# Shared expert's split weights kept on chip, matmul operands placed modulo 512 bytes, and later sends in a fused two-layer kernel

## The chip, the core and the metric

The kernel runs on one NeuronCore of one Trainium2 chip. The metric is device time in microseconds (us) of one execution. A core has a matrix engine (TensorE, PE in the profile; its weight loads are PEld), a vector engine (VectorE, DVE), a scalar engine (ScalarE, ACT), GpSimd (POOL) and SyncE (SP). The last three also issue DMA transfers, each in its own queue. Each engine works through its own queue in order and waits for semaphores of the others. On-chip memory has 128 partitions; a matmul reads a stationary operand of 128x128 and a moving one of up to 512 columns from it, and writes to PSUM.

## The reference

`x` is 32 sequences of 128 tokens with 512 features. Two layers, each a "cond" part that feeds an "ffn" part:

```
# layer 0, cond: mixture of experts with one shared expert
shared = (silu(x @ sw1.T) * (x @ sw3.T)) @ sw2.T            # hidden 1024
s      = sigmoid(x @ router_w.T + t_emb @ router_t_w.T)     # 8 experts, best 2 of them
routed = sum over the 2 chosen: gate * (gelu(x @ rw1[e].T) @ rw2[e].T)   # hidden 256
hid    = (shared + routed) / 3
# layer 0, ffn: each sequence picks one of 8 experts from its last token
sel    = argmax(softmax(gelu(hid[:, -1] @ Wp1 + bp1) @ Wp2 + bp2))
x1     = x + hid + 0.3 * ((gelu(hid @ W1[sel] + b1) @ W2[sel] + b2) @ Wo + bo)
# layer 1, cond: token shift, 16 experts by a hash of the token id, capacity 256 each
xk, xr = x1 + (shift(x1) - x1) * maa_k,  x1 + (shift(x1) - x1) * maa_r
y      = relu(buf @ w_key[e])**2 @ w_value[e], gathered back
r      = sigmoid(xr @ w_recept.T)
# layer 1, ffn: a gated recurrence over the 32 sequences (batch: 128 positions)
c      = sigmoid(z@wf.T + c@uf.T + bf) * c + sigmoid(z@wi.T + c@ui.T + bi) * tanh(z@wc.T + c@uc.T + bc)   # z = r * y
out    = x1 + tanh(z @ wo.T + c_final @ uo.T + bo)
```

All of it is float32.

## The kernel before, in words

**Matmuls in three terms.** Every float32 operand of a large matmul is split into a high part (a cast on ACT, L62) and a low part (a subtraction on DVE, L63), by `split`. `mm3` (L65 to L74) then issues three matmuls for each 128 of the contraction: high·high, high·low, low·high. So a product over 512 features is 12 matmuls.

**Stages, in order of time.** (1) *Shared expert, groups 0 to 3*: a group is 4 sequences, 512 tokens. `shared` (L193) loops over units `n`, eight per group (one per 128 of the hidden 1024): `up(n)` makes two products of 12 matmuls with 512 columns (`p`, from `xhl` and `swu`), `down(n - 1)` 12 matmuls into four accumulators (`acc`, from `swd` and `as`). For each unit the three raw weights are fetched by SP (`fetch_sw`, 256 KB each, tiles `swr`) two units ahead and split (`split_sw`) one unit ahead into two rotating buffers, although the same eight units of weights come round in each group. Router, top-2 choice and slot numbers run beside it. (2) *Routed experts*: 71 blocks of 128 gathered tokens; `r_up` (`pur`, 12 matmuls of 256 columns), `turn_h`, `r_down` (`por`, 6 of 512), with the split weights `r1`, `r2` (64 KB per partition each) in the right-hand memory. Near its end (`i == NBLK - 10`, block 61) the first `x` and the first two weight units of the next stage are fetched and split. (3) *Shared expert, groups 4 to 7*: the same loop (`shared` again, L926), with `combine` for finished sequences between (`sums`): POOL gathers two routed rows (`o`), DVE adds, PE transposes (`pth`), ACT scales. In group 7 DVE runs `policy` (which expert each of the first 24 sequences takes), POOL gathers the first expert weights (`fetch_w`, tiles `rawB`), and `split_w` splits them into four tiles `wB_W1a`, `wB_W1b`, `wB_W2a`, `wB_W2b`.

(4) *The sequences' experts*: the loop at L1131, one sequence per iteration, in order of their expert, so that weights change seldom. PE does `up` in two halves (`pu`), `bend` (transposes and gelu), `turn_r` (transposes of the sequence before into `rT`), and `down` in two halves (`po`). Every second iteration a pair of sequences is closed: `close(c)` multiplies with `Wo` (`pb`, 48 matmuls of 256 columns), forms `x1`, `dx`, `xk`; `mix_r(c)` makes `xr`. `send_k(b)` transposes `xk` and stores its rows, `send_v(b)` multiplies `xr` with `w_recept` (`pv`, 12 matmuls) and stores the result. (5) *16 experts*: `phD` (256 columns, from `xe` and `wD`) and `poD` (512 columns, from `wD` and `hD`). (6) *Recurrence*: 32 steps, each with three products of the state (`uc`, `ui`, `uf` with `cT`), three of the input (`wc`, `wi`, `wf` with `z`) and a part of the output product (`poF`).

**Where tiles lie.** Tile pools are stacks: left-hand pools grow up from the constants, right-hand pools down from the top of the memory. The last constant is `pad`, 64 bytes (L137). `shifted` (L56) gives a tile 128 bytes more than it needs and starts its use 64 bytes in; `xb`, `rT` and `xe`, which meet 256-column matmuls, are made by it.

**Order in queues.** The program's order is the base; the tile framework's planner then orders each engine's queue by its own costs and due times, so work that isn't ready in its plan is placed behind other work. `reuse_waits="tile"` makes a new tile wait for the last users of the bytes it takes.

Of the kernel before, what the change touches and what calls it, by code (L numbers as in the profile page):

```python
# [42 lines left out]
LINE = 128 // 4  # L43
SHIFT = LINE // 2


@with_exitstack
def tile_kernel(ctx: ExitStack, tc: tile.TileContext, a: dict, out: bass.AP):
# [7 lines left out]
    def shifted(pool, n, **kw):  # L56

        return pool.tile([P, n + LINE], FR, **kw)[:, SHIFT : SHIFT + n]

# [77 lines left out]
    pad = const.tile([P, SHIFT], F32, name="pad")  # L137
# [7 lines left out]
    with ExitStack() as sa:  # L145
        kw = dict(reuse_waits="tile")
        raw_p = sa.enter_context(tc.tile_pool(name="raw_p", bufs=6, **kw))
        swu = sa.enter_context(tc.tile_pool(name="swu", bufs=2, **kw))
        swd = sa.enter_context(tc.tile_pool(name="swd", bufs=2, **kw))
        xh = sa.enter_context(tc.tile_pool(name="xh", bufs=KD, **kw))  # L150
        xgp = sa.enter_context(tc.tile_pool(name="xgp", bufs=3, **kw))
# [6 lines left out]

        NSW = KF * NG
        sw_raw, sw_hl, x_raw, xhl = {}, {}, {}, {}  # L160

        def fetch_sw(n, which=range(3)):
            if n < NSW:
                sw_raw.setdefault(n, {}).update(
                    {i: fetch(a["sw"][n % KF, i], f"swr_{n}_{i}") for i in which}
                )

        def split_sw(n, which=range(3)):
            if n < NSW:
# [23 lines left out]
        def shared(groups, pools, hook, done, mid=None, before_last=None, more=False):  # L193
# [36 lines left out]
            for n in range(first, last + 1):  # L230
# [11 lines left out]
                if c == KF - 2 and (g < groups[-1] or more):  # L242
                    fetch_x(g + 1)
# [7 lines left out]
        with ExitStack() as s0:  # L251
# [22 lines left out]
            s1, ps_x, ps_u = ExitStack(), None, None  # L274
            srt = s0.enter_context(ExitStack())
# [304 lines left out]
            def hook2(g, c):  # L580
# [4 lines left out]
                if g == 1 or (g == 2 and c < 5):  # L585
# [3 lines left out]
                    if g == 2 and c == 4:  # L589
# [5 lines left out]
                        r12.append(rw_p.tile([P, 2, E0 * RCOL], FR, name="r1"))  # L595
                        r12.append(rw_p.tile([P, 2, E0 * RCOL], FR, name="r2"))
# [30 lines left out]
        with s1:  # L627
# [37 lines left out]
            for i in range(NBLK + 1):  # L665
# [8 lines left out]
                if i == NBLK - 10:  # L674
                    with tc.issue_after(stored):
                        fetch_x(NG // 2)
                    split_x(NG // 2)
                    fetch_sw(NSW // 2)
                    split_sw(NSW // 2)
                    fetch_sw(NSW // 2 + 1)  # L680

        srw.close()

        wh = sw_.enter_context(tc.tile_pool(name="wh", bufs=1, side="right", **kw))
# [143 lines left out]
        ws = {k: wh.tile([P, 2, KD, D], FR, tag="w" + k, name=f"wB_{k}") for k in ("W1a", "W1b", "W2a", "W2b")}  # L828
# [23 lines left out]
        def split_w(i):  # L852

            if i < len(todo):
                raw = raws.pop(i)
                kind, b = order[todo[i]]
                if b not in (0, PARTS[0]) and b not in changed:
# [12 lines left out]
        with ExitStack() as s2:  # L870
            tp = s2.enter_context(tc.tile_pool(name="tp2", bufs=2, **kw))
# [57 lines left out]
    with ExitStack() as sb:  # L929
# [4 lines left out]
        wb = sb.enter_context(tc.tile_pool(name="wb", bufs=1, **kw))  # L934
        sc = sb.enter_context(ExitStack())
# [20 lines left out]
        seqs = {}  # L956
# [68 lines left out]
        def turn_r(b):  # L1025
# [5 lines left out]
            if j == 0:  # L1031
                rT = shifted(bp, 2 * KD * PB * P, tag="rT", name=f"rT_{c}")
                rTs[c] = rT.rearrange("p (h k q) -> p h k q", h=2, k=KD)
# [9 lines left out]
        def close(c, last=False):  # L1043
# [4 lines left out]
            x1 = bp.tile([P, -(-n1 // LINE) * LINE], F32, tag="x1", name=f"x1_{c}")  # L1048
# [42 lines left out]
        def mix_r(c, pool, tag):  # L1091
# [6 lines left out]
            xrs[c] = pool.tile([P, 2, KD, PB, P], FR, tag=tag, name=f"xr_{c}")  # L1098
# [32 lines left out]
        for b in range(-1, NB + 1):  # L1131
# [25 lines left out]
            if b + 1 < NB:  # L1157
                bend(b + 1, "a")
                up(b + 1, "b")
                used()  # L1160
            if late == GB and step == 2:
                sc.close()
                end_p = sb.enter_context(tc.tile_pool(name="end_p", bufs=1, **kw))
            if b == NB:
                send_v(NB - 6)
            if j == PB - 1 and 0 <= c < NB // PB:
# [6 lines left out]
            if 0 <= b < NB:  # L1173
                down(b, "b")
                used()
            if b + 1 < NB:
                bend(b + 1, "b")
            if 0 <= b - 2 < NB - 2:
                send_k(b - 2)
                if b - 2 < NB - 6:  # L1180
                    send_v(b - 2)
# [488 lines left out]
```

## Time and profile before

| | |
|---|---|
| median of 3 runs | 2561.73 us (2558.79 to 2566.84) |
| the profiled execution | 2564.9 us, of it span 2563.2 us |
| granted TensorE clock, mean | 0.988 |
| PE busy in the span | 2480.9 us |
| DMA moved | 370.01 MB |

| stage | us from the span's start |
|---|---|
| 1 shared expert, groups 0 to 3 | 5 to 307 |
| 2 routed experts | 307 to 558 |
| 3 shared expert, groups 4 to 7 | 558 to 863 |
| 4 sequences' experts | 863 to 1495 |
| 5 16 experts | 1495 to 1867 |
| 6 recurrence and output | 1867 to 2563 |

The stages are cut at the first matmul of each kind in the timeline of PE. A row of a timeline gives start, duration, engine, line, operation, out<-in, shape and count, and in brackets how long the engine had been idle and what ended that. A row of the waits gives the waiting group, the group waited for, the total in us, how often, and the longest. Matmuls are pipelined: the distance from one start to the next is what one costs, and the duration in a row is longer than that. A name in the profile has its numbers left out.

### The profile page before, as it was taken

The page shows a single profiled execution, that of the slowest core. Times are in us where ns is not written, and L with a number is a line of the kernel's source. Part 1 is how long each engine was busy: PE and PEld are TensorE (multiplying, and loading weights), DVE is VectorE, ACT ScalarE, POOL GpSimd, SP SyncE. Part 2 cuts the span into 40 slices and gives each one's busy share as a digit, 9 for nine tenths or more (in the row PEclk, how much of TensorE's full clock was granted, in tenths as well). Part 3 has the DMA queues.
Part 4 walks back from the last instruction along what each step waited for, and adds up shares of the span by engine and source line. Part 5 has one row for each costly group of instructions (what it writes and reads, how often), then busy time and mean ns, then how long its engine had stood idle before and what let it go on. Part 6 is the DMA issues. An engine that isn't in the chain of part 4 may idle for free. (4 is left out here: it accounts for less than half of the span.)

```text
span 2563.2 us, 37388 instructions
## 1 busy us (share of the span) xinstructions
PE 2480.9 (97%) x13044; PEld 2076.7 (81%) x13044; DVE 1374.6 (54%) x2413; ACT 1104.7 (43%) x2007; POOL 437.8 (17%) x459
## 2 busy tenths in 40 slices
PE   8999999999997998999999999999999999999996
PEld 5788899987876787888887889999978888888885
DVE  7797655557767544445454477667643332333336
ACT  5445533344445544455455466666532222222214
POOL 1000022222323223333222110000010000000003
PEclk9999999999998999999999999999999999999998
DMA  5445544477777324333243287776451111111027
GB/s 179 161 132 176 169 155 151 155 230 244 268 255 246 119 87 128 100 117 111 81 139 120 93 280 241 230 228 223 140 168 42 38 37 37 37 42 46 25 74 267
DMA packets 203487, 370.01 MB, mean 144 GB/s; under 512 B 38625, under 2 KB 73489, under 8 KB 200225
## 3 DMA queue, kind: packets, MB, share of 16 engines
q1 hardware_dynamic: 151872, 263.30, 30.6%
q0 software_dynamic: 36160, 74.90, 9.9%
q10 hardware_dynamic: 15264, 29.37, 3.1%
q8 instruction: 108, 1.77, 0.3%
q14 instruction: 83, 0.67, 0.1%
HBM read 392.81 MB, written 88.13 MB: 188 GB/s over the span
## 5 line engine op out<-in xcount | busy, mean ns | idle before, releaser
L70 PE MATMUL p<-xhl,swu 128*128 128x512 f32 x1536 | 380.7, 401 | 17.9 <-DVE sg L211 7.7
L70 PEld LDWEIGHTS p<-xhl,swu 128*128 128x128 f32 x1536 | 290.4, 192 | 81.6 <-issue 8.1
L63 DVE TENSOR_TENSOR wD<-rawD,wD 128x1024 fp32r<-128x1024 f32 x128 | 156.5, 1229 | 78.6 <-ACT wD L62 78.5
L70 PE MATMUL acc<-swd,as 128*128 128x512 f32 x768 | 188.2, 392 | 2.1 <-ACT as L62 1.2
L70 PEld LDWEIGHTS phD<-xe,wD 128*128 128x128 f32 x1536 | 184.5, 190 | 1.3
L70 PE MATMUL phD<-xe,wD 128*128 128x256 f32 x1536 | 185.2, 281 | 0.0
L70 PE MATMUL poD<-wD,hD 128*128 128x512 f32 x768 | 182.7, 393 | 0.0
L70 PEld LDWEIGHTS acc<-swd,as 128*128 128x128 f32 x768 | 143.6, 188 | 34.3 <-ACT as L62 2.1
L70 PEld LDWEIGHTS poD<-wD,hD 128*128 128x128 f32 x768 | 142.0, 188 | 29.6 <-DVE hD L63 0.4
L62 ACT CAST wD<-rawD 128x1024 fp32r<-128x1024 f32 x128 | 133.1, 1047 | 55.3 <-PE poD L70 30.7
L255 POOL DMA_INDIRECT xg<-in_x_rows_dram,blk_t x71 | 67.5, 951 | 466.1 <-PE ptx L265 261.6
L1352 POOL DMA_INDIRECT y<-res_d,gat_i x32 | 32.3, 1009 | 583.1 <-DVE r L1371 504.1
L70 PE MATMUL por<-r,hbr 128*128 x426 | 117.7, 410 | 3.0 <-ACT hbr L62 2.9
L70 PE MATMUL pur<-r,xb 128*128 x852 | 118.7, 288 | 0.2
L63 DVE TENSOR_TENSOR xb<-ptx,xb 128x512 fp32r<-128x512 f32 x71 | 49.1, 691 | 112.6 <-ACT xb L62 112.6
L62 ACT CAST swu<-swr 128x512 fp32r<-128x512 f32 x128 | 75.0, 620 | 79.4 <-PE p L70 52.6
L70 PEld LDWEIGHTS pur<-r,xb 128*128 128x128 f32 x852 | 105.6, 189 | 2.0 <-ACT xb L62 0.6
L70 PE MATMUL pv<-w_recept_hl,xr 128*128 128x512 f32 x384 | 100.2, 406 | 5.9 <-DVE xr L63 5.9
L708 POOL DMA_INDIRECT o<-o_d,s_i x64 | 78.8, 1232 | 150.8 <-DVE swu L63 28.8
L70 PE MATMUL ps_f<-wf_hl,z 128*128 128x512 f32 x384 | 98.0, 402 | 1.7 <-ACT wf_hl L62 0.8
L70 PE MATMUL ps_c<-wc_hl,z 128*128 128x512 f32 x384 | 96.6, 399 | 0.7 <-ACT z L62 0.7
L70 PEld LDWEIGHTS pb<-rT,Wo_hl 128*128 128x128 f32 x768 | 92.8, 188 | 4.7 <-DVE rT L1037 3.2
(1005 smaller groups left out, 4856.8 us busy)
## 6 DMA issues: line engine op xcount, KB each, us to landing
swr<-in_sw_dram SPq DMA_DIRECT2D x192, 256.0 KB
rawD<-in_w_key_dram SPq DMA_DIRECT2D x64, 512.0 KB
rawD<-in_w_value_dram SPq DMA_DIRECT2D x64, 512.0 KB
o_d<-obr SPq DMA_DIRECT2D x71, 256.0 KB
xraw<-in_x_dram SPq DMA_DIRECT2D x32, 256.0 KB
rraw<-in_rw_dram SPq DMA_DIRECT2D x32, 256.0 KB
xc<-in_x_dram SPq DMA_DIRECT2D x32, 256.0 KB
hid_d<-o ACTq DMA_DIRECT2D x32, 256.0 KB
```

The costliest lines, as they stand in the source:

```text
L62: nc.scalar.copy(hi, src)
L63: return nc.vector.tensor_tensor(lo, src, hi.bitcast(F32), ALU.subtract).ins
L70: done = nc.tensor.matmul(ps, lhsT=left(hl, k), rhs=right(hr, k), start=start and k + n == 0, stop=stop and 3 * k + n == last,)
L255: nc.gpsimd.indirect_dma_start(out=xg[i], out_offset=None, in_=a["x_rows"], in_offset=bass.IndirectOffsetOnAxis(ap=blk_t[:, i : i + 1], ax ...
L708: nc.gpsimd.indirect_dma_start(out=o[n], out_offset=None, in_=o_d, in_offset=bass.IndirectOffsetOnAxis(ap=idx[:, b : b + 1], axis=0),)
L1352: nc.gpsimd.indirect_dma_start(out=y, out_offset=None, in_=res_d, in_offset=bass.IndirectOffsetOnAxis(ap=gat_i[:, b : b + 1], axis=0),)
```

## The change

Three things. **Kept weights**: in group 4 the split weights of the eight units go into four tiles `kept_u` and two tiles `kept_d`, and groups 5 to 7 read them there; no weight is fetched or split after unit 39. `kept_u` takes the four slots that the sequences' weights (`wB_*`) take over later, tile by tile; `kept_d` has a pool of its own on the right. `swu` and `swd` exist in stage 1 alone. `x` of groups 6 and 7 is fetched at `c == 3`, not 6. The first `x` of stage 3 is fetched at block 55, not 61, and the first kept weights are split after stage 2, not in it. `r2` is allocated ahead of `r1`, so they change places. **Addresses**: `pad` has 448 bytes, `shifted` adds 512 bytes and starts 64 bytes in, `x1` and `rT` get pools of their own behind the others. **Later sends**: `close` and `mix_r` stand at the end of the iteration, and both sequences of a pair are sent in the iteration after it, their pieces between `up`, `down` and `bend`.

```diff
-LINE = 128 // 4
-SHIFT = LINE // 2
+LINE, SHIFT, RIGHT = 512 // 4, 64 // 4, 480 // 4
...
-    def shifted(pool, n, **kw):
-        return pool.tile([P, n + LINE], FR, **kw)[:, SHIFT : SHIFT + n]
+    def shifted(pool, n, by=SHIFT, **kw):
+        return pool.tile([P, n + (LINE if by == SHIFT else by)], FR, **kw)[:, by : by + n]
...
-    pad = const.tile([P, SHIFT], F32, name="pad")
+    pad = const.tile([P, 448 // 4], F32, name="pad")
...
-        swu = sa.enter_context(tc.tile_pool(name="swu", bufs=2, **kw))
-        swd = sa.enter_context(tc.tile_pool(name="swd", bufs=2, **kw))
...
-        xgp = sa.enter_context(tc.tile_pool(name="xgp", bufs=3, **kw))
+        sxg = sa.enter_context(ExitStack())
+        xgp = sxg.enter_context(tc.tile_pool(name="xgp", bufs=3, **kw))
...
         NSW = KF * NG
+        KEPT = KF * (NG // 2)
...
         def fetch_sw(n, which=range(3)):
-            if n < NSW:
+            if n < KEPT + KF:
...
         def split_sw(n, which=range(3)):
-            if n < NSW:
+            if n >= KEPT:
+                c = n % KF
+                if n < KEPT + KF:
+                    if c % 2 == 0:
+                        kept_u[c // 2] = wh.tile([P, 2, 2, 2, KD, P], FR, tag="w", name=f"kept_u{c}")
+                    if c % 4 == 0:
+                        kept_d[c // 4] = dn_p.tile([P, 4, 2, D], FR, tag="d", name=f"kept_d{c}")
+                sw_hl[n] = kept_u[c // 2][:, c % 2], kept_d[c // 4][:, c % 4]
+            if n < KEPT + KF:
...
-                if c == KF - 2 and (g < groups[-1] or more):
+                if c == (KF - 2 if n < KEPT + KF else 3) and (g < groups[-1] or more):
                     fetch_x(g + 1)
...
-                        r12.append(rw_p.tile([P, 2, E0 * RCOL], FR, name="r1"))
-                        r12.append(rw_p.tile([P, 2, E0 * RCOL], FR, name="r2"))
+                        r12[:] = [rw_p.tile([P, 2, E0 * RCOL], FR, name=n) for n in ("r2", "r1")][::-1]
...
-                if i == NBLK - 10:
+                if i == NBLK - 16:
                     with tc.issue_after(stored):
                         fetch_x(NG // 2)
+                if i == NBLK - 10:
                     split_x(NG // 2)
-                    fetch_sw(NSW // 2)
-                    split_sw(NSW // 2)
-                    fetch_sw(NSW // 2 + 1)
+                    fetch_sw(KEPT)
+                    fetch_sw(KEPT + 1)
+        sxg.close()
         srw.close()
-        wh = sw_.enter_context(tc.tile_pool(name="wh", bufs=1, side="right", **kw))
+        wh = sw_.enter_context(tc.tile_pool(name="wh", bufs=4, side="right", **kw))
...
-        ws = {k: wh.tile([P, 2, KD, D], FR, tag="w" + k, name=f"wB_{k}") for k in ("W1a", "W1b", "W2a", "W2b")}
+        ws = {}
...
+                if b == 0:
+                    ws[kind] = wh.tile([P, 2, KD, D], FR, tag="w", name=f"wB_{kind}")
...
+            dn_p = s2.enter_context(tc.tile_pool(name="dn_p", bufs=2, side="right", **kw))
+            split_sw(KEPT)
+            pad2 = dn_p.tile([P, 320 // 4], F32, bufs=1, name="pad2")
+            nc.gpsimd.memset(pad2, 0.0)
...
+        x1p = sb.enter_context(tc.tile_pool(name="x1p", bufs=1, **kw))
+        rTp = sb.enter_context(tc.tile_pool(name="rTp", bufs=1, **kw))
...
-                rT = shifted(bp, 2 * KD * PB * P, tag="rT", name=f"rT_{c}")
-                rTs[c] = rT.rearrange("p (h k q) -> p h k q", h=2, k=KD)
+                rTs[c] = rTp.tile([P, 2, KD, PB * P], FR, tag="rT", name=f"rT_{c}")
...
-            x1 = bp.tile([P, -(-n1 // LINE) * LINE], F32, tag="x1", name=f"x1_{c}")
+            x1 = x1p.tile([P, n1 - n1 % LINE + SHIFT], F32, tag="x1", name=f"x1_{c}")
...
-            xrs[c] = pool.tile([P, 2, KD, PB, P], FR, tag=tag, name=f"xr_{c}")
+            if pool is not end_p:
+                xrs[c] = pool.tile([P, 2, KD, PB, P], FR, tag=tag, name=f"xr_{c}")
+            else:
+                xr = shifted(pool, 2 * KD * PB * P, LINE - SHIFT, tag=tag, name=f"xr_{c}")
+                xrs[c] = xr.rearrange("p (h k b q) -> p h k b q", h=2, k=KD, b=PB)
...
             if b + 1 < NB:
                 bend(b + 1, "a")
+            pair = b - 3 if b % 2 and 0 <= b - 3 < NB - 2 else None
+            if pair is not None:
+                send_k(pair)
+            if b + 1 < NB:
                 up(b + 1, "b")
                 used()
...
+            if pair is not None:
+                send_k(pair + 1)
             if b == NB:
                 send_v(NB - 6)
+            if 0 <= b < NB:
+                down(b, "b")
+                used()
+            if pair is not None and pair < NB - 6:
+                send_v(pair)
+            if b + 1 < NB:
+                bend(b + 1, "b")
+            if pair is not None and pair < NB - 6:
+                send_v(pair + 1)
             if j == PB - 1 and 0 <= c < NB // PB:
                 wo_done, k_done = close(c, b == NB)
                 fetch_xh(c + 1)
...
-            if 0 <= b < NB:
-                down(b, "b")
-                used()
-            if b + 1 < NB:
-                bend(b + 1, "b")
-            if 0 <= b - 2 < NB - 2:
-                send_k(b - 2)
-                if b - 2 < NB - 6:
-                    send_v(b - 2)
...
-            mix_r(NB // PB - 1, bp, "rT")
+            mix_r(NB // PB - 1, rTp, "rT")
```

More of the change, by code (lines that the diff above doesn't have):

```diff
@@ L159, in tile_kernel @@
         NSW = KF * NG
+        KEPT = KF * (NG // 2)
         sw_raw, sw_hl, x_raw, xhl = {}, {}, {}, {}
+        kept_u, kept_d = {}, {}
         def fetch_sw(n, which=range(3)):
-            if n < NSW:
+            if n < KEPT + KF:
                 sw_raw.setdefault(n, {}).update(
@@ L274, in tile_kernel @@
             s1, ps_x, ps_u = ExitStack(), None, None
+            swu = s0.enter_context(tc.tile_pool(name="swu", bufs=2, **kw))
+            swd = s0.enter_context(tc.tile_pool(name="swd", bufs=2, **kw))
             srt = s0.enter_context(ExitStack())
@@ L954, in weight_b @@
             return pair
-        seqs = {}
+        seqs, end_p = {}, None
         def seq(p):
```

## The prediction

> **What bounds the kernel now.** I read the page's busy times first, then who waited for whom on TensorE, then the timeline of single stages. The page:
>
> ```profile
> PE 2480.9 (97%) x13044; PEld 2076.7 (81%) x13044; DVE 1374.6 (54%) x2413; ACT 1104.7 (43%) x2007; POOL 437.8 (17%) x459
> ```
>
> TensorE (PE) is the bound all through; the other engines matter only where PE waits for them. So a gain has two sources: a shorter matmul, or a PE wait that goes. Matmul spacing first, in one step of the last recurrence (start, duration, group):
>
> ```profile
> 2102.78 2.88 PE L70 MATMUL ps_c<-uc_hl,cT 128*128 128x512 f32 x12
> 2105.50 2.88 PE L70 MATMUL ps_i<-ui_hl,cT 128*128 128x512 f32 x12
> 2108.22 2.95 PE L70 MATMUL ps_f<-uf_hl,cT 128*128 128x512 f32 x12
> 2111.01 2.96 PE L70 MATMUL ps_c<-wc_hl,z 128*128 128x512 f32 x12
> 2113.81 2.97 PE L70 MATMUL ps_i<-wi_hl,z 128*128 128x512 f32 x12
> ```
>
> Same shape, but start to start the first two take 2.72 us per 12 (226.7 ns each), uf 2.79, wc 2.80. What differs is the addresses, which follow from adding up the tiles. Left-hand pools begin at 20064, 96 modulo 512; right-hand pools end at 229344, 480. uc, ui and cT are left (96 and 96); uf and the three input weights are right (480 against 96).
>
> PE's waits in the second shared stage (557.8 to 863.3 us):
>
> ```profile
> PE p L70 <- DVE sg L211: 7.7, 1, 7.7
> PE p L70 <- DVE xhl L63: 3.4, 2, 2.1
> PE pth L728 <- ACT o L730: 3.1, 1, 3.1
> ```
>
> and among the sequences' experts (863 to 1495 us):
>
> ```profile
> PE pv L70 <- DVE xr L63: 5.9, 2, 3.0
> PE ptB L1105 <- DVE xk L1059: 4.7, 3, 2.1
> PE pb L70 <- DVE rT L1037: 3.0, 1, 3.0
> ```
>
> They cost more than they last. PE in the first:
>
> ```profile
> 770.38 0.47 PE L70 MATMUL p<-xhl,swu 128*128 128x512 f32 x1
> 772.96 4.32 PE L70 MATMUL p<-xhl,swu 128*128 128x512 f32 x11 [2.11 <-DVE xhl L63]
> 780.35 1.12 PE L728 MATMUL pth<-ident,o 128*128 128x128 f32 x4 [3.06 <-ACT o L730]
> 781.12 3.91 PE L70 MATMUL p<-xhl,swu 128*128 128x512 f32 x12
> 784.86 1.52 PE L70 MATMUL acc<-swd,as 128*128 128x512 f32 x6
> ```
>
> 11 matmuls in 4.32 us: after a wait, seven to ten run at 427 ns, half clock. From 770.38 to 784.86 are 14.5 us for two groups of 12 and four transposes, worth 5.8: 8.7 us lost. Behind it, on ScalarE (ACT) and GpSimd (POOL):
>
> ```profile
> 771.07 0.62 ACT L62 CAST xhl<-xraw 128x512 fp32r<-128x512 f32 x1 [3.71 <-DMA xraw<-in_x_dram]
> ...
> 778.66 0.62 ACT L62 CAST swu<-swr 128x512 fp32r<-128x512 f32 x1 [3.30 <-DMA swr<-in_sw_dram]
> ...
> 821.89 1.05 ACT L62 CAST wB_W1a<-rawB 128x1024 fp32r<-128x1024 f32 x1 [8.21 <-DMA rawB<-in_W1a_dram,idxw]
> 814.74 1.62 POOL L837 DMA_INDIRECT rawB<-in_W1a_dram,idxw  x1 [0.31 <-DVE condS L804]
> ```
>
> ACT stands in order before a transfer, and what PE needs is queued behind. At 821.89 that transfer is the first sequence's weights, gathered once VectorE (DVE) has finished the policy; with the half clock 12.8 us go between 814.8 and 832.0.
>
> **The change, 1: addresses.** The pad of 448 for 64 bytes moves the left pools from 96 to 480. Every tile behind it is a multiple of 512 or, with x1 and rT, comes last, so 512-column operands agree. Per 12 matmuls the recurrence gains 0.07 (uf), 0.08 (wc), 0.09 (wi) and 0.05 (wf: 2.88 against 2.83 for poF, both behind transposes): 0.29 x 32 steps = 9.3 us. Among the sequences' experts (weights 480, activations 96 or 352; timeline from 1050 to 1067) groups take 2.77 to 2.79, 2.88 behind transposes, against 2.72 and 2.83: 0.055 x 128 = 7.0. Routed down (por, mean start to start 232.4 ns against about 227.5): 426 x 5 ns = 2.1. The value matmuls that use the left-hand pool in the 16-expert stage: 256 x 5 = 1.2. Together 19.6.
>
> The 256-column matmuls keep a difference, now 64 bytes. phD at a difference (stationary less moving) of 448 takes 117.8 ns today, at 320 116.6; it loses 0.8 us. pb stays at 117.8. pur gets +64, which the trace does not have: between 116.2 (its own at 320) and 119.4 (11 matmuls at 128), I take 117.8, a loss of 0.6, ends -0.3 and +2. Net gain 18.
>
> Here a rule speaks against the change. The Trainium skill (TensorE: Matmul & The Clock Gate, Step-by-step) says loading the next weights steals no read bandwidth from the running matmul, and (Back-to-back issue gap) puts N=512 at N/2.4 + 2.5, 216 ns, with no address in it. By it part 1 is worth 0. The rows have 227 and 233 ns on one shape, so the measurement decides: 18.
>
> **2: kept weights.** 72 fetches of 256 KB (18.9 of the stage's 73 MB, DMA share 0.76 to 0.80 in its first 210 us) and 72 casts on ACT (620 ns) and DVE (686 ns) go: 45 and 49 us, beside PE, so worth nothing by themselves. What counts is the waits. The loss at 770: x comes at c=3 into idle buffers, no swr is waited for: 8 of 8.7. The small ones at 611 to 738 (5.7 together, late x and late gathers of o): 4. The 12.8: DVE runs without a gap from 786 to 818 with 7 of these splits in it (4.4 us); the gathers leave about that much earlier and share the engines with less. What is late next is the same cast; I leave 5 and count 7.5. Sum 19.5.
>
> Added: the first kept tile lies where r1 lay (hence the swapped order), so its cast and subtraction (0.6 + 0.7) now follow the last pur instead of lying in the routed stage. PE has there one por group (1.4) and two transposes, and today fills the wait for the last hbr with three p matmuls; 1 us lost, bounds 0 and 3. kept_d waits for the last por, but its reader comes two units (some 11 us of p matmuls) later. POOL's pad2 memset waits for r2 too, with the gathers of o behind it; those wait for o_d anyway. Two of the sequences' weights now wait for kept slots: W2a (cast at 828 today) for the p matmuls of c=5, some 7 us more, W2b (853) for those of c=7, some 5. Behind them stand casts that the planned order can put first, and their readers start at 875 and later: 0, or 5 where a cast is placed badly. Net 18.5.
>
> x fetched 6 routed blocks (6 x 3.5 us) earlier takes ACT's 4.75 us wait at 528 away, which costs PE 2.85 and about 2 of half clock: 4. SP issues the same transfers there; two sets of weights queue behind the split of x as now, with obr stores behind them, and those have slack.
>
> **3: later sends.** No instruction is added. Today close ends in mix_k and mix_r (1.2 + 1.9 + 1.7 us DVE, then xr's cast and subtraction) and send_k follows at once. Now a pair is sent in the next iteration, around down and up groups of 2.8 us each. The two pv waits (3.1 and 1.4 of half clock each) and three ptB waits (2.3, 2.3, 0.8) total 14.4; the rT wait 3.1 (close moves behind two more groups): 13 of 17.5. Queues: ACT's rows copies and SP's stores of xk, v and x1 move along; the stores of x1 and the fetch of the next xB go some 4 us later, with more than an iteration (15 us) in hand. The last pair keeps its order, so the expert stage starts no later.
>
>
> Sum: 18 + 18.5 + 4 + 13 = 53.5. Queue orders are planned anew, and each wrongly placed cast costs 3 to 5 us; I give back 6.5 for one or two. 47 from the profiled execution's 2564.9 is 2517.9; that execution is 3.2 above the median of the three, so 2515 in their terms.
>
> **Rivals.** *Waits come back elsewhere* (0.20): the pv and pb stalls arose because DVE waited for ACT's casts of new weights, and those stay; so may the 8.2 us wait. Then 18 + 10 + 2 = 30: 2532. *The address modulo 512 isn't the cause* (0.19): every slow 512-column group of this trace has one operand from the left pools and one from the right, every fast one has both from one side, so the side itself would explain the same rows, and the new addresses leave the sides as they are. Then 47 - 18 = 29: 2533. For: 23 pv matmuls at 352 and 96, both left and 256 apart, run at 226.7. Against: nothing but that addresses a few hundred bytes apart are the smaller assumption. *A wait per pair* (0.05): xk, dx, x1 and xr have one buffer, and the sends hold xk and xr longer; if the next close waits for them in all 15 pairs at today's 3.1 + 1.4, that costs 68 against 47: 2583. It decides above 3.1 us per pair. Against it, send_v ends a whole iteration before the next close. *Nothing moves* (0.03).
>
> **Numbers.** The likeliest case has 0.53, with 2500 to 2528 of its own. The range 2498 to 2543 takes in both middle rivals and most of their joint case. A difference under about 0.3% (8 us) can't be told from none: faster 0.91, within 0.04 (nothing moves, and the weakest of the middle cases), slower 0.05.
>
> **What would show it.** uf, wc, wi and pu, po groups at 2.72 us per 12 as uc now; if they stay at 2.79, part 1 fails. No swr after 640 us, DMA share down after it, and a second shared stage of about 286 us for 305; if ACT still stands 8 us before W1a, 7.5 are missing. No PE wait for xr or xk. The forecast is wrong if pur goes past 120 ns or each pair shows a new wait.

## The result, and the profile after

The changed kernel takes 2535.36 us (median of 4 runs, 2534.52 to 2537.62) against 2560.93 us for the kernel before, measured beside it. The ratio is 0.9901, with a 95% interval of 0.9888 to 0.9913. It is faster by 25.6 us, where 47 were forecast; the range 2498 to 2543 holds it. The two profiled executions stand 29.7 us apart (spans 2563.2 and 2533.5), because that of before lies 4 us above its median and that of after on it. The experiments ran on several chips, on some of which the kernel before takes 2567 or 2569 us, so what is compared below are ratios to it.

The page's busy line, to be set beside the one of before:

```profile
PE 2460.9 (97%) x13044; PEld 2077.8 (82%) x13044; DVE 1332.4 (53%) x2341; ACT 1064.2 (42%) x1935; POOL 428.5 (17%) x460
```

The number of matmuls is the same and PE is busy 20 us less; the 72 casts on ACT and the 72 subtractions on DVE are gone. By stage, cut at the first matmul of each kind, in the two profiled executions:

| stage | before, us | after, us | difference |
|---|---|---|---|
| 1 shared expert, groups 0 to 3 | 301.3 | 300.3 | -1.0 |
| 2 routed experts | 251.2 | 249.2 | -2.0 |
| 3 shared expert, groups 4 to 7 | 305.5 | 292.4 | -13.1 |
| 4 sequences' experts | 631.5 | 627.6 | -3.9 |
| 5 16 experts | 372.2 | 371.6 | -0.6 |
| 6 recurrence and output | 696.3 | 686.9 | -9.4 |

In the traces below, a stage that no edit touches moves from one execution to the next: stage 1 by up to 6 us, stage 2 by 5, stage 3 by 4, stages 4 to 6 by 1 to 2. So one profile measures stages 4 and 6 well, and stages 1 and 2 badly.

**Stage 6** came as forecast (9.4 us here; 7.7 to 9.4 with the stage times of the other runs whose addresses agree modulo 256). The timeline of one recurrence step after (start, duration, group):

```profile
2080.84 2.88 PE L71 MATMUL ps_i<-ui_hl,cT 128*128 128x512 f32 x12
2083.56 2.88 PE L71 MATMUL ps_f<-uf_hl,cT 128*128 128x512 f32 x12
2086.28 2.88 PE L71 MATMUL ps_c<-wc_hl,z 128*128 128x512 f32 x12
2089.00 2.89 PE L71 MATMUL ps_i<-wi_hl,z 128*128 128x512 f32 x12
```

uf, wc and wi now start 2.72 us behind one another, as uc and ui did before.

**Stage 3** lost its large stalls. PE's timeline where 8.7 us were lost before, ACT at the first cast of the sequences' weights, and PE behind it:

```profile
769.66 3.01 PE L71 MATMUL p<-xhl,kept_u 128*128 128x512 f32 x12
772.51 0.60 PE L742 MATMUL pth<-ident,o 128*128 128x128 f32 x4
772.87 3.01 PE L71 MATMUL p<-xhl,kept_u 128*128 128x512 f32 x12
775.72 2.88 PE L71 MATMUL acc<-kept_d,as 128*128 128x512 f32 x12
...
806.59 2.00 ACT L63 CAST wB_W1a<-rawB 128x1024 fp32r<-128x1024 f32 x2 [2.75 <-DMA rawB<-in_W1a_dram,idxw]
806.98 5.07 PE L71 MATMUL p<-xhl,kept_u 128*128 128x512 f32 x21
814.08 0.73 PE L71 MATMUL acc<-kept_d,as 128*128 128x512 f32 x2 [2.04 <-ACT as L63]
815.97 4.10 PE L71 MATMUL acc<-kept_d,as 128*128 128x512 f32 x10 [1.16 <-DVE as L64]
819.87 5.71 PE L71 MATMUL p<-xhl,kept_u 128*128 128x512 f32 x24
```

The groups from 769 to 778 run without a gap. ACT stands 2.75 us before the gathered weights, not 8.21. Behind it 12 matmuls take from 811.7 (21 x 0.227 after 806.98) to 819.9, 8.1 us for 2.7: 5.4 lost where it had been 12.8, now in waits for `as`, which ACT casts behind the gathered weights. A new loss has come at the stage's start, though. DVE and PE there, around 570 us:

```profile
566.73 2.88 PE L71 MATMUL acc<-kept_d,as 128*128 128x512 f32 x12
571.60 0.75 DVE L738 SCALAR_TENSOR_TENSOR o<-o,g,shc 128x512 f32<-128x512 f32 x1 [3.79 <-DMA o<-o_d,s_i]
573.67 0.66 PE L742 MATMUL pth<-ident,o 128*128 128x128 f32 x4 [4.06 <-DVE o L739]
```

DVE waits 3.79 us for routed rows, which are gathered while the weights of the last kept units are fetched; PE loses 4.2 us and, at half clock (427 ns for a matmul of 512 columns), some 1.8 more.

**Stage 4** is where the forecast gain is missing. The longest of PE's waits there after:

```profile
PE pt_0b L1028 <- ACT ue_0b L1021: 7.9, 1, 7.9
PE pt_6a L1028 <- ACT o L744: 2.6, 1, 2.6
PE ptB L1130 <- ACT hf_26a L1031: 2.4, 1, 2.4
PE ptB L1130 <- ACT hf_16a L1031: 2.3, 1, 2.3
```

No wait for xr, xk or rT is left, but PE now waits 7.9 us for ue_0b at the stage's start, where it had waited 2.8, and up to 2.6 for ACT in several pairs. ACT's timeline at that place, before and then after:

```profile
869.91 1.05 ACT L62 CAST Wo_hl<-raw_Wo 128x1024 fp32r<-128x1024 f32 x1 [3.04 <-DMA sh_d<-shc]
```

```profile
858.81 1.04 ACT L63 CAST Wo_hl<-raw_Wo 128x1024 fp32r<-128x1024 f32 x1 [7.86 <-DMA sh_d<-shc]
```

The cast of Wo, which nobody reads for another 40 us, stands first in ACT's queue. By the trace it waits for the store of the shared expert's rows, whose bytes its tile takes over; the gelu of the first sequence and the copy ue_0b are queued behind it.

### The profile page after: what moved, and what is told of

Same layout as the page of the kernel before. It is cut to its first block, busy times and chain, and to the rows that moved or that the text cites. A ratio compares the mean times of both kernels' runs of the same rounds, so it can differ in the third digit from the quotient of the medians.

```text
span 2533.5 us, 37051 instructions
## 1 busy us (share of the span) xinstructions
PE 2460.9 (97%) x13044; PEld 2077.8 (82%) x13044; DVE 1332.4 (53%) x2341; ACT 1064.2 (42%) x1935; POOL 428.5 (17%) x460
## 5 line engine op out<-in xcount | busy, mean ns | idle before, releaser
L71 PE MATMUL p<-xhl,swu 128*128 128x512 f32 x768 | 189.0, 397 | 5.3 <-ACT xhl L63 5.3
L71 PE MATMUL p<-xhl,kept_u 128*128 128x512 f32 x768 | 185.6, 397 | 0.7 <-DVE kept_u L64 0.7
L71 PEld LDWEIGHTS p<-xhl,swu 128*128 128x128 f32 x768 | 144.7, 191 | 36.5 <-ACT xhl L63 5.6
L71 PEld LDWEIGHTS p<-xhl,kept_u 128*128 128x128 f32 x768 | 143.3, 190 | 30.5 <-DVE kept_u L64 1.1
L71 PE MATMUL pur<-r,xb 128*128 x852 | 117.8, 287 | 0.9 <-ACT xb L63 0.4
L71 PE MATMUL acc<-kept_d,as 128*128 128x512 f32 x384 | 96.1, 400 | 5.1 <-DVE as L64 3.1
L71 PE MATMUL poF<-z,wo_hl 128*128 128x512 f32 x384 | 96.5, 399 | 0.0
L71 PE MATMUL acc<-swd,as 128*128 128x512 f32 x384 | 95.0, 392 | 0.0
L71 PE MATMUL pb<-rT,Wo_hl 128*128 128x256 f32 x768 | 94.6, 281 | 0.0
```

The source lines that it names most:

```text
L71: done = nc.tensor.matmul(ps, lhsT=left(hl, k), rhs=right(hr, k), start=start and k + n == 0, stop=stop and 3 * k + n == last,)
```

## The experiments

Each edit is against the changed kernel. Stage times are from one profiled execution each.

**1. Is it the address, and modulo what?** pad320 and pad192 change one constant: the left-hand pools start 128 and 256 bytes away from the right-hand ones, modulo 512. Nothing else differs, neither the sides of the memory nor the order of queues.

```diff
-    pad = const.tile([P, 448 // 4], F32, name="pad")
+    pad = const.tile([P, 320 // 4], F32, name="pad")   # pad192: 192 // 4
```

> The changed kernel with a pad of 320 bytes for 448: left-hand tiles lie at 352 modulo 512, right-hand ones stay at 480, so every 512-column matmul with one operand from each side (4954 of them) has its operands 128 bytes apart. Theory (the distance modulo 512 sets the spacing): those matmuls go from about 228 ns back to about 233, so some 20 to 25 us more, about 2558, with uf, wc, wi groups at 2.79 to 2.81 us per 12 instead of 2.72. Rival (the faster spacing comes from the new order of work or from something else in the change, not from the address): no change, 2535 within 4.

> The changed kernel with a pad of 192 bytes: left-hand tiles at 224 modulo 512, right-hand ones at 480, so mixed 512-column operands are 256 bytes apart. If operands have to agree modulo 512, it costs what 128 bytes apart costs, about 2558. If agreement modulo 256 is enough (before the change 23 pv matmuls at 352 and 96 ran at 226.7 ns), 2535 within 4 and groups at 2.72 us per 12.

pad320: ratio 0.9955 (0.9943 to 0.9967), some 14 us slower than the changed kernel. pad192: 0.9900 (0.9886 to 0.9913), the same as the changed kernel. The recurrence, pad320 and then pad192:

```profile
2079.96 2.96 PE L71 MATMUL ps_f<-uf_hl,cT 128*128 128x512 f32 x12
2082.75 2.96 PE L71 MATMUL ps_c<-wc_hl,z 128*128 128x512 f32 x12
2085.55 2.97 PE L71 MATMUL ps_i<-wi_hl,z 128*128 128x512 f32 x12
```

```profile
2086.58 2.88 PE L71 MATMUL ps_f<-uf_hl,cT 128*128 128x512 f32 x12
2089.30 2.88 PE L71 MATMUL ps_c<-wc_hl,z 128*128 128x512 f32 x12
```

2.79 and 2.80 again with operands 128 bytes apart, 2.72 with 256 apart. So the distance is the cause, not the side of the memory, and for these matmuls agreement modulo 256 is enough: 0 and 256 bytes are fast, 128 and (before) 384 slow. Of pad320's loss, 8.4 us lie in stage 6 (695.3 against 686.9) and 4.6 in stage 3 (297.0 against 292.4): the kept weights lie on the right, so stage 3 needs the agreement too, which before, with weights and activations both on the left, had it for nothing. A stage 3 timeline of pad320 shows it (acc is kept_d with as, p is kept_u with xhl):

```profile
647.29 5.82 PE L71 MATMUL p<-xhl,kept_u 128*128 128x512 f32 x24
652.95 2.95 PE L71 MATMUL acc<-kept_d,as 128*128 128x512 f32 x12
655.74 0.60 PE L742 MATMUL pth<-ident,o 128*128 128x128 f32 x4
```

24 and 12 matmuls start 5.66 and 2.79 us before what follows; the same groups of the changed kernel take 5.57 and 2.72 to 2.73.

20 to 25 us were expected of pad320, and 14 came. Stage 4 did not pay: its 512-column matmuls went back from 234.8 to 237.5 ns in the mean, 5.1 us in all, but the stage took 628.0 us for 627.6, because PE waited 1.1 us less and lost 2.8 us less at half clock. Whether slower matmuls shorten these waits or chance did, one profile doesn't say. So in stage 4 the addresses' worth is shown in PE's spacing, not in time.

**2. What are the later sends worth?** addr_kept has the addresses and the kept weights, with the loop's order of before:

```diff
-            pair = b - 3 if b % 2 and 0 <= b - 3 < NB - 2 else None
-            if pair is not None:
-                send_k(pair)
...
+            if 0 <= b < NB:
+                down(b, "b")
+                used()
+            if b + 1 < NB:
+                bend(b + 1, "b")
+            if 0 <= b - 2 < NB - 2:
+                send_k(b - 2)
+                if b - 2 < NB - 6:
+                    send_v(b - 2)
```

> The changed kernel with the sequences' loop of before: new addresses and kept weights, but close, send_k and send_v where they stood. If the later sends are worth the 13 us of the prediction, this takes about 2548. Theory from the trace after (new waits of transposes for ScalarE give most of it back, the stage is only 4 us shorter and the spacing alone explains 5): 2535 to 2540.

Ratio 0.9918 (0.9904 to 0.9931), so the sends bring 0.0017, some 4.4 us, with intervals that overlap; in the profile stage 4 is 636.7 us against 627.6, 9.1 us (3.2 of them at half clock; the table below has the parts). PE's waits of addr_kept in stage 4:

```profile
PE pt_0b L1028 <- ACT ue_0b L1021: 7.5, 1, 7.5
PE pv L71 <- DVE xr L64: 5.9, 2, 2.9
PE ptB L1130 <- DVE xk L1080: 5.3, 3, 2.0
PE pb L71 <- DVE rT L1058: 3.1, 1, 3.1
```

The three waits of before are back (5.9, 4.7 and 3.0 there), so the later sends did remove them: 14.3 us here. The waits for hf and o shown above took most of their place. And the 7.5 for ue_0b is here as well (6.8 in pad320): it came with the kept weights and their layout, not with the sends and not with the distance of operands.

**3. Three waits of the changed kernel, each attacked alone.** mixr_late puts `mix_r` into the next iteration, ahead of `send_k`, because the cast of xr stood in front of hf in ACT's queue and waited there 2.4 us for DVE:

```diff
             if pair is not None:
+                mix_r(pair // PB, bp if pair // PB < NB // PB - 2 else end_p, "xr")
                 send_k(pair)
...
-                if c < NB // PB - 2:
-                    mix_r(c, bp, "xr")
-                elif c == NB // PB - 2:
-                    mix_r(c, end_p, "xr")
```

> The changed kernel with mix_r of a pair moved from behind its close into the next iteration, in front of send_k of the pair. Theory: with the close at the end of an iteration, ScalarE's cast of xr waits some 2 us for VectorE's mix and stands in front of the casts that free the transposes' buffers; PE then waits 0.3 to 2.6 us per pair, 10.3 in all, with about 3 of half clock behind the long ones. Moved, these waits go: 2523 to 2530. Rival: the casts of new weights and the chain of rT hold ScalarE anyway, and the waits stay: 2533 to 2537.

Ratio 0.9860 (0.9844 to 0.9876), an interval wholly under that of the changed kernel; but stage 4 of its profile took 627.3 us, as before the edit. Two things must be known here. First, the planner put xr's cast in front of hf again, in 12 of 14 pairs; only its own wait shrank, from between 2.0 and 3.3 us to 0.4 or none. ACT of the changed kernel, and then of mixr_late, at the same pair:

```profile
1143.43 1.05 ACT L63 CAST xr<-dx 128x1024 fp32r<-128x1024 f32 x1 [2.39 <-DVE dx L1116]
1144.38 1.99 ACT L63 CAST wB_W2a<-rawB 128x1024 fp32r<-128x1024 f32 x2
...
1146.54 1.13 ACT L1031 ACTIVATE hf_16a<-pt_16a,b 128x128 f32<-128x128 f32 x4
```

```profile
1154.29 1.05 ACT L63 CAST xr<-dx 128x1024 fp32r<-128x1024 f32 x1
...
1155.50 1.14 ACT L1031 ACTIVATE hf_16a<-pt_16a,b 128x128 f32<-128x128 f32 x4
```

Second, the execution that was profiled took the longest of its four: 2542.3 us at a mean granted clock of 0.985, where the other three took 2530.3 to 2533.9 at 0.989 to 0.991. So this profile can't speak against the timed ratio. Two more runs below have the edit in them.

wo_late moves the call of `weight_b("Wo")` to the end of its iteration, first_late moves two combines of stage 3 back by one unit, and three is mixr_late with both. They ran beside after_again, the changed kernel once more.

```diff
-            if b == 0:
-                wo0 = weight_b("Wo")
-            if b == 1:
-                wrec = weight_b("w_recept")
...
             if b + 1 < NB:
                 bend(b + 1, "b")
+            if b == 0:
+                wo0 = weight_b("Wo")
+            if b == 1:
+                wrec = weight_b("w_recept")
```

The edit of first_late:

```diff
-                    n += (g == last - 1 and c == KF - 1) - (g == h and c == 0)
+                    n += (g == last - 1 and c >= KF - 2) - (g == h and c < 2)
```

> The changed kernel itself, on the same chip as the three edits of this call, so that they have it beside them. Both theories: 0.990 of the kernel before, as in its first measurement (0.9901). If it differs by more than 0.002, differences under that between calls say nothing.

> The casts of Wo and of w_recept are issued at the end of the first two iterations of the sequences' stage instead of in their middle; nothing else changes. Theory: at the start of that stage ScalarE stands 7.9 us in front of Wo's cast, whose transfer waits for the stores of the shared expert's rows, and the cast of the first up projection's output is queued behind it; with Wo later TensorE's wait of 7.9 us and about 1.7 us of half clock behind it go, less what the weights of the first sequence themselves still need: 6 to 9 us less than the changed kernel (ratio 0.987 to 0.988), the sequences' stage at 619 to 622 us for 627.6. Rival: the stall belongs to the transfers that crowd at the boundary, and the wait moves to the next transfer in order (the next sequence's weights or Wo at the first use by the closing of the pair): within 3 us of the changed kernel (0.989 to 0.991).

> In the second shared stage the first two combines of routed rows come one unit later than in the changed kernel; nothing else changes. Theory: the first combine's gathered rows land late, because the last weights of the shared expert (units 34 and up) are now fetched only at the stage's start, together with them; one unit (some 6 us) more covers the wait of 4.2 us and most of the half clock behind it: 4 to 6 us less than the changed kernel (ratio about 0.988), the second shared stage at 287 to 288 us for 292.4. Rival: the late transfer is that of the weights themselves, or the postponed combine meets the next one: the stage stays within 2 us of 292.4 and the ratio at 0.990.

> Both of these edits, and the mixing of each pair's receptance input moved into the next iteration, behind the casts that the next up projection needs. Theory: three separate waits, so the gains add up: 6 to 9 and 4 to 6 us of the other two runs, and 3 to 5 for the receptance input (the waits of 2.3 us for hf and the small ones at every pair): 13 to 20 us less than the changed kernel, ratio 0.982 to 0.985. Rival for the third edit: its profile alone showed the sequences' stage unchanged at 627.3 us, so that it is worth 0: ratio 0.985 to 0.987. If two of the three give nothing: 0.988.

after_again: 0.9900 (0.9886 to 0.9915). wo_late: 0.9890 (0.9873 to 0.9907), stage 4 at 626.6 us for after_again's 627.0. It changed nothing, since the planner put the cast back where it had been, in front of the first gelu; in ACT's timeline of wo_late:

```profile
863.90 1.04 ACT L63 CAST Wo_hl<-raw_Wo 128x1024 fp32r<-128x1024 f32 x1 [7.07 <-DMA raw_Wo<-in_Wo_dram]
```

So it told nothing of the worth of the edit, only how far apart two runs of nearly one order can come out, 0.001, and that in this run the load of Wo itself landed no earlier than the store.

first_late: 0.9890 (0.9873 to 0.9906), stage 3 at 290.0 for after_again's 288.5. The wait moved. In stage 3 of first_late:

```profile
PE acc L71 <- DVE as L64: 4.9, 3, 3.6
...
PE pth L742 <- DVE o L739: 0.6, 1, 0.6
```

DVE still stands 3.78 us before the same gathered rows (at 574.95), now with `as` queued behind it, so the rival holds. three: 0.9870 (0.9853 to 0.9888). Its profile has stages 3 and 4 at 289.1 and 627.2 us, but it again caught the longest of four executions (2539.1 us at 0.986; the others 2531.6 to 2534.9 at 0.989 to 0.991), so it can't tell where the 0.003 lies.

**4. The wait at the start of stage 4, with the order forced.** wo_forced ties Wo's cast and subtraction behind those of the first sequence's second hidden half (`bent` keeps these two instructions), on their own engines; both_forced also ties mixr_late's cast behind the first hidden half; x_old puts the fetches of x back to their old places.

```diff
             if b == 0:
-                wo0 = weight_b("Wo")
+                with tc.issue_after(bent[0, "b"][0]), tc.issue_after(bent[0, "b"][1]):
+                    wo0 = weight_b("Wo")
```

```diff
             if pair is not None:
+                with tc.issue_after(bent[b + 1, "a"][0]) if b + 1 < NB else nullcontext():
+                    mix_r(pair // PB, bp if pair // PB < NB // PB - 2 else end_p, "xr")
                 send_k(pair)
...
-                if c < NB // PB - 2:
-                    mix_r(c, bp, "xr")
-                elif c == NB // PB - 2:
-                    mix_r(c, end_p, "xr")
```

The edit of x_old:

```diff
-                if c == (KF - 2 if n < KEPT + KF else 3) and (g < groups[-1] or more):
+                if c == KF - 2 and (g < groups[-1] or more):
                     fetch_x(g + 1)
...
-                if i == NBLK - 16:
+                if i == NBLK - 10:
                     with tc.issue_after(stored):
                         fetch_x(NG // 2)
-                if i == NBLK - 10:
                     split_x(NG // 2)
```

> Wo's cast and subtraction are tied behind the first sequence's second hidden half on ScalarE and VectorE (the planned order had put the cast back in its old place when only the line was moved). Theory: ScalarE no longer stands 7 to 8 us before the gelu of the first sequence; TensorE's wait of 7.1 us for pt_0b and the half clock behind it (about 1.7) go, and Wo is not read before the first pair is closed some 40 us later: the sequences' stage at 618 to 621 us for 627.0, ratio 0.9865 to 0.9875. Rival: the transfers crowd at the boundary whatever waits for them, and the next cast in order (hidhl or the next W2a) waits instead: the stage at 625 to 628, ratio 0.989 to 0.991.

> As wo_forced, and the mixing of each pair's receptance input (DVE's four operations, the cast and the subtraction of xr) goes into the next iteration, its cast tied behind the first hidden half of that iteration. Theory: in the changed kernel the cast of xr waits some 2 us for VectorE ahead of hf, which the transposes of xk then wait for (2.4, 2.3, 0.7 us and small ones in other pairs); with hf first these go: 4 to 7 us less than wo_forced (0.984 to 0.985) and the stage at 612 to 616. Rival: the 2.3 us waits are those of two sequences whose new weights are cast there (1.99 us each), not of xr; then within 2 us of wo_forced.

> The changed kernel with the fetches of x at their old places: the first of the second shared stage at block 61 of the routed stage, those of groups 6 and 7 at unit 6 of the group before. Kept weights, addresses and sends as in the changed kernel. Theory (the forecast's): the earlier x in the routed stage is worth 4 us, and x for group 7 was waited for at 770 us because six transfers of weights stood in the queue ahead of it, which the kept weights remove: 4 to 6 us more than the changed kernel, ratio 0.9917 to 0.9925, the second shared stage within 3 us of 290. Rival: the kept weights are not what ends the stall at 770, the earlier x is: then the stall of 8.7 us comes back as well and the second shared stage is at 296 to 299, ratio 0.994 to 0.996. If neither matters: 0.990.

wo_forced: 0.9887 (0.9869 to 0.9905), stage 4 at 623.6 us, between the two expectations. The wait shrank and changed its name; PE and DVE of wo_forced:

```profile
864.14 0.63 PE L71 MATMUL po<-wB_W2a,hb_0a 128*128 128x512 f32 x2
867.62 0.75 DVE L738 SCALAR_TENSOR_TENSOR o<-o,g,shc 128x512 f32<-128x512 f32 x1 [12.21 <-DMA shc<-sh_d]
869.08 0.69 DVE L1034 TENSOR_TENSOR hb_0a<-hf_0a,hb_0a 128x512 fp32r<-128x512 f32 x1
869.82 4.64 PE L71 MATMUL po<-wB_W2a,hb_0a 128*128 128x512 f32 x10 [5.05 <-DVE hb_0a L1034]
```

With ACT free, DVE stands in the way in the same manner: the combine of a late sequence, which the program issues five iterations later and the planner had drawn forward, waits 12.2 us for shared rows on their way through memory, and the low part of hb_0a is queued behind it.

both_forced: 0.9878 (0.9859 to 0.9897), stage 4 at 623.5 us. xr's cast went behind hf in all 14 pairs and PE's waits for hf are gone, but PE waits for DVE's rT in their place (4.8 us in three waits), so tied in this way the edit of `mix_r` is worth nothing. What it is worth as in mixr_late (0.9860) and three (0.9870), where two timed ratios say some 0.003 and the profiles caught the wrong execution, stays open.

x_old: 0.9895 (0.9878 to 0.9911), the same as the changed kernel. Stage 3 took 291.9 us and the stall at 770 did not come back, so of these two the kept weights ended it. In the routed stage the wait of before did come back:

```profile
531.51 2.70 PE L71 MATMUL por<-r,hbr 128*128 x6 [3.22 <-ACT hbr L63]
534.01 0.63 PE L664 MATMUL pth<-ident,ge 128*128 128x128 f32 x2
534.41 2.60 PE L71 MATMUL pur<-r,xb 128*128 x12
```

3.22 us and, by the spacing of the two groups behind (2.50 and 2.44 for about 1.47 each), 2 of half clock: 5 in the trace, which the timed runs don't show. The runs with the earlier x explain why: PE waits in the routed stage there too, for xb, ge and hbr, 1.6 to 4.2 us in all, against 3.7 in x_old. One wait became several smaller ones.

**5. Both queues freed.** clear_start is wo_forced with the combine tied behind a later hidden half:

```diff
             if 0 <= late < GB and step == 2:
-                combine(NB - GB + late, ps_t)
+                with tc.issue_after(bent[b - 3, "b"][0]), tc.issue_after(bent[b - 3, "b"][1]):
+                    combine(NB - GB + late, ps_t)
```

> As wo_forced, and the first combine of a late sequence (VectorE's two operations on rows and shared rows that come back from memory, planned three iterations early) is tied behind the third sequence's hidden half. Theory: in wo_forced VectorE stood 12.2 us before that combine with the low part of the first hidden half queued behind it, which is the 5.0 us wait that was left (with 1.8 us of half clock behind it); with both moved TensorE is not held at the start of the stage: 5 to 7 us less than wo_forced, the sequences' stage at 617 to 619 us for 623.6 and 627.0, ratio 0.9855 to 0.987. Rival: a third cast or load in order (the next sequence's hidden rows, the next gathered weights) waits for the same crowded transfers: the stage at 622 to 625, ratio 0.988 to 0.989.

Ratio 0.9853 (0.9829 to 0.9877), stage 4 at 617.5 us, span 2523.6: as the theory had it (617 to 619). It beats both kernels, and its interval lies wholly under that of the changed kernel. PE at the start of stage 4:

```profile
852.47 1.87 PE L71 MATMUL pu_0b<-wB_W1b,hidhl 128*128 128x512 f32 x7
854.17 1.76 PE L71 MATMUL pu_1a<-wB_W1a,hidhl 128*128 128x512 f32 x7
855.78 0.60 PE L1028 MATMUL pt_0b<-ident,ue_0b 128*128 128x128 f32 x4
856.13 1.40 PE L71 MATMUL pu_1a<-wB_W1a,hidhl 128*128 128x512 f32 x5
857.37 2.91 PE L71 MATMUL po<-wB_W2a,hb_0a 128*128 128x512 f32 x12
```

No wait is left. The transfers are as crowded as ever. The stretch of 17 us from the stage's start, in the windows of the changed kernel and then of clear_start (span, then busy us of PE, PEld, DVE, ACT and POOL, granted clock, DMA share, GB/s):

```profile
847.00:864.00 17.00, 9.13 (x44) 7.37 (x43) 3.54 (x7) 6.71 (x12) 4.63 (x6) 0.81 0.85 280
```

```profile
848.00:865.00 17.00, 17.00 (x82) 14.03 (x81) 5.73 (x10) 13.03 (x27) 7.03 (x8) 1.00 0.93 301
```

PE is busy 17.0 of 17 us at a DMA share of 0.93, where it was busy 9.1 at 0.85. In this stretch the crowd alone cost PE nothing (its first 12 matmuls start 2.72 us before the next group); two instructions that waited for it at the head of a queue did.

## Why the prediction was right and wrong

The direction and the range held, and the address rival fell. The likeliest case missed: by 17 us in the profiled executions (29.7 for 47), by 21 in the medians (25.6), outside its own 2500 to 2528. The range held because it had been drawn to take in the rivals too.

**Addresses, 18: right in PE's spacing, not shown in the time of stage 4.** Stage 6 gave 9.4 for 9.3; its spacings explain some 8 of it. The forecast took poF as the measure for groups behind transposes, and poF itself went from 2.83 to 2.85 us per 12 while wf went from 2.88 to 2.85. In stage 4 the mean spacing of 512-column matmuls (those under 340 ns) fell from 238.2 to 234.8 ns, times 1878 is 6.4 us for 7.0, but pad320 had this spacing back in stage 4 and lost only 0.4 us there. The 16-expert stage gave 0.6 for 0.4, within its scatter. por moved only from 232.4 to 231.2 ns in its undisturbed part, 0.5 us for 2.1. pur at a distance of 64 took 116.7 ns, inside its bounds, below the 117.8 taken. Counted by time, the addresses paid 9 to 10 us, and up to 17 if the spacing of stage 4 is counted in full. The Trainium skill's gap for N=512 (TensorE: Matmul & The Clock Gate, Back-to-back issue gap), which that section gives for an isolated matmul, has no address in it and gives 0 for this part. The rows have 226.7 ns and, 128 bytes apart, 233.6 for one shape, and pad320 lost 14 us by the addresses alone (8.4 in stage 6, 4.6 in stage 3, where the kept weights had made them matter), so the measurement decides.

**Kept weights, 18.5: 2 to 5 too much in stage 3 (13.1 in the profile, 17.0 in that of after_again), and 5 more in stage 4.** The stall at 770 went whole (8 forecast), and at the first sequence's weights 5.4 are left where 5 were left by the forecast. The small waits did not shrink by 4: at the stage's start a new one of 4.2 and 1.8 arose, because weights that used to be split in the routed stage are now fetched beside the first gathers of o (read from the trace; first_late shows that the rows come late, not why). The named failure is the line on late slots, "0, or 5 where a cast is placed badly", of which 0 was taken. W2b's cast waits for the slot of the last kept tile; in the changed kernel the next gather follows it:

```profile
841.94 1.05 ACT L63 CAST wB_W2b<-rawB 128x1024 fp32r<-128x1024 f32 x1 [2.12 <-PE p L71]
846.25 1.20 POOL L851 DMA_INDIRECT rawB<-in_W1a_dram,idxw  x1 [14.49 <-DVE wB_W2b L64]
```

That gather left 1 us before the stage's end, where it had left 6 before it, and joins the stores of the shared rows; ACT's wait for those grew from 3.04 to 7.86 us. wo_forced and clear_start show that a badly placed cast and a badly placed combine turn it into PE time. That the later gather is what made the stores late is read from the two traces and was not tried by itself.

**Earlier x, 4: not shown.** x_old has the wait in its trace, not in its time, since smaller waits stand there in the other runs. The forecast put nothing in the place of the wait that went.

**Later sends, 13: too large.** 9 by profile and 4 by time, against addr_kept. The waits that went were the ones named; the step that failed is that nothing was put in their place. PE's waits inside stage 4, without its start and its end, sum to 14.7 us before and 12.2 after, now of transposes for hf, o and a branch on DVE. The give-back of 6.5 had the right kind, a cast placed in front of what PE needs (xr's, shown above), but it is only part of what came back.

By stage then, stage 2 was to give 5.5 and gave 2.0, stage 3 18.5 and 13.1, stage 4 20 and 3.9; the give-back of 6.5 covered part. Where stage 4's gain went can be summed from the traces. "Half clock" is what matmuls lose that take over 1.5 times their usual spacing, "spacing" what the other 512-column ones take above 226.7 ns:

| stage 4, us | before | after | addr_kept | pad320 | clear_start |
|---|---|---|---|---|---|
| the stage | 631.5 | 627.6 | 636.7 | 628.0 | 617.5 |
| PE's waits | 21.8 | 23.7 | 26.1 | 22.6 | 17.0 |
| half clock | 11.5 | 13.7 | 16.9 | 10.9 | 10.1 |
| spacing | 21.6 | 15.3 | 17.0 | 20.4 | 15.6 |

From before to after, the spacing gave 6.3 us, and waits and half clock took 4.1 back. At the stage's start they took 5.7 more (PE's gap and the half clock behind it, 3.0 and 1.7 before, 8.0 and 2.4 after), so in all the rest of the stage they fell by 1.6 us only, where 13 were forecast. That is the missing 16: 5.7 at the start and 11.4 of the sends, less about 1 that other matmuls gained. Some of the 11.4 may be the shorter matmuls' doing, as pad320 has 3.9 less of both. addr_kept lost 5.4 us more at half clock than the kernel before, with nearly the same waits inside the stage (15.4 and 14.7), and the record doesn't say why; the timed intervals allow the sends anything from 0 to 9 us against it.

The rival "waits come back elsewhere", at 2532, described the outcome better than the likeliest case: it had 30 us, the profiles have 29.7. It had named casts of new weights on ACT as what stays, and such a cast is behind one of the three longest new waits inside the stage (`wB_W2a`, 1.99 us in front of hf_16a). That its sum fits so closely is partly luck, since its waits for xr and rT did go and others came.

## What to carry to other kernels

When a change takes waits away from the bounding engine, list what stands next in each in-order queue and ask what each of those instructions waits for: work that nobody needs for 40 us, at the head of a queue before a late transfer, costs as much as a missing operand. When time and profile disagree, compare the profiled execution with the others of its set first. A freed or reused buffer moves the transfers behind it, so look at the next stage's start as well as at the stage edited. Moving a call in the source is no experiment while a planner orders the queues; tie the order explicitly and see in the timeline that it moved.

## What was not expected of the hardware

- 512-column matmuls whose operands lie 256 bytes apart modulo 512 run as fast as aligned ones (wc 226.8 ns in pad192 and in the changed kernel); 128 apart (pad320) they take 233.6, 384 apart (before) 233.7. The forecast had only the modulus of 512.
- 256-column matmuls do not follow this: pur took 116.7 ns at 64 apart in the changed kernel and 115.7 in addr_kept, 116.1 at 320 (pad192) and 118.0 at 448 (pad320). Two runs at one distance differ by 1 ns, so only the last stands out.
- A DMA share of 0.93 with ACT, DVE and POOL at work did not slow PE by any measurable amount (17.0 us busy of 17 at a granted clock of 1.00), while one stall of 7.9 us drew the clock of the same stretch down to 0.81.
- Not every wait is paid twice. In the kernel before, the 2.96 us wait for xr at 962.6 us is followed by matmuls at 427 ns, but only from the seventh on; the 3.03 us wait for rT at 992.6 is followed by none. After the change a wait of 1.93 us (601.1) is followed by seven. The forecast's half clock behind a wait is what these waits had cost in one execution.
